# Fetching query and key blocks with fewer, wider DMAs, the first keys by halves, and a reordered start of a decoder layer on one core

## The chip, the core and the metric

The kernel runs on one core of one Trainium2 chip. The time is the device time of one execution in microseconds (us), the median of three runs. A core has TensorE (PE, matrix products), VectorE (DVE), ScalarE (ACT), GpSimd (POOL) and SyncE (SP), which here only issues DMAs. Each engine executes its instructions in its own fixed order, and waits for others by semaphores; an instruction that waits holds all that stand behind it. DMAs are issued by an engine's queue and carried out by 16 DMA engines.

## The reference, cut to what matters

One decoder layer in fp32 on x of shape (4, 1024, 256): self-attention, cross-attention on a context of 64 rows, and a feed-forward block with ternary weights, each behind a layer normalisation and with a residual. The change touches the self-attention alone:

```python
x = x + attn(layernorm(x))
# attn: 16 heads of width 16
q, k, v = split(x @ W_qkv + b_qkv)
energy = einsum('bqhe,bkhe->bqhk', q, k)
out = softmax(energy) / sqrt(256) @ v
out = out @ W_out + b_out
```

## The kernel before, in words

Self-attention is cut into 16 units: 4 batch rows of 1024 tokens, each with 4 groups of 4 heads. A unit takes the heads of its group in two pairs.

**Projection.** `ln1` (L324) normalises a batch's tokens and transposes them to xnT. `project(b, c)` (L341) makes q and k of half of the heads for one batch, in eight pieces of 256 columns (for the very first, four of 512). Each value is kept as two summands (a rounded part by ScalarE, L359, and the rest by VectorE, L360, together in a tile hl, of which there are two buffers), and each finished half of 512 tokens is written to device memory (kept_q, kept_k; 512 KB a write, L365).

**Fetch.** `fetch(u)` (L368) reads back what unit u needs. For each pair there is a tile q and a tile k of 128 partitions by 1024 tokens. The partitions hold, for each of two heads n, four blocks of 16 rows: for q the parts 0, 0, 1, 1 and for k the parts 0, 1, 0, 1, so that one product over 64 rows gives the sum of all four cross terms. `parts` (L380) issues one DMA for each block of 16 rows, so eight for a tile and 32 for a unit, on SP's queue. For unit 0, q comes in halves of 512 columns and four of the eight key blocks of each pair go by ScalarE's queue.

**Maxima and scores.** `maxima(u)` (L412) computes the energies once to find each row's maximum: for a tile of 128 queries, a pair and a half of the keys (kh), two matmuls into two banks of the ring of 7, then two VectorE reductions `mx` (L433). There are 64 reductions a unit. `turn_maxima` transposes them to mT. `scores` (L872) then computes the energies again, transposed, subtracts the maximum by a second matmul, and ScalarE takes the exponential (L888); `weigh` (L796) multiplies by v.

**Order.** The main loop (L891) has 16 steps a unit. A step issues scores of both pairs, two steps of the maxima (`top`), the weighing of the step before, and what `fill` picks from three lines of other work (`due`: layernorms, projections and values of later batches; `later`; `aside`), each with a number of pieces and a due time from which it gets credit. So the maxima run ahead: those of unit u+1 begin at step 6 of unit u, and need its second pair from the middle of step 7. Unit u+1 is fetched in steps 0 and 1 of unit u (L921 to L926), one pair a step. The maxima of the first half of unit 0 run ahead of the loop (L861), beside the values of batch 0 and the first two pieces of `project(0, 1)`. Ahead of them stands the start: x of batch 0 in four loads, wq and wk, the first layernorm, `project(0, 0)`, `fetch(0)`.

TensorE's matmuls and SP's DMAs are kept in program order (`ordered`, L54). For the other engines the framework's scheduler picks the order. In the first layernorm it puts VectorE's statistics of all eight token tiles (L233, L234) ahead of the first normalisation (L256).

Of the kernel before, what the change touches and what calls it, by code (L numbers as in the profile page):

```python
# [9 lines left out]
F32 = mybir.dt.float32  # L10
# [11 lines left out]
P = 128  # L22
# [8 lines left out]
def decoder_layer(ctx, tc, a, out):  # L31
# [24 lines left out]
    def matmul(*args, **kwargs):  # L56
        ordered(nc.tensor.matmul(*args, **kwargs))  # L57
# [4 lines left out]
    def dma(**kwargs):  # L62
        ordered(nc.sync.dma_start(**kwargs))
# [4 lines left out]
    x_of = {}  # L68
    x_slots = [const.tile([P, NT, E], F32, name=f"x{i}") for i in range(3)]

    def load_x(b, n=1, view=x_view, slot=None):
        step = NT // n
        x_of[b] = x_slots[b % 3 if slot is None else slot]
        for i in range(n):
# [20 lines left out]
    def load_row(name, cols=E):  # L95
        t = const.tile([P, cols], F32, name=name)
        nc.gpsimd.dma_start(out=t, in_=a[name].partition_broadcast(P))
        return t

    load_x(0, 4)  # L100
    wqk = []
    for name in ("wq", "wk"):

        wide = main.tile([P, E // P, H, 32], F32, tag="q", name=f"{name}_in", bufs=4)
        dma(out=wide, in_=a[name].rearrange("(c p) (h e) -> p c h e", p=P, e=32))
        t = const.tile([P, E // P, H, D], F32, name=name)
        nc.gpsimd.tensor_copy(t, wide[:, :, :, 1 : 1 + D])
        wqk.append(t.rearrange("p c h e -> p c (h e)"))
# [10 lines left out]
            )  # L119
        bqk[name] = t  # L120
    wv = load_w("wv", E, late=True)
    bo = load_row("bo")
    xbv = load_row("xbv")
    xbo = load_row("xbo")

    ident = const.tile([P, P], F32, name="ident")
    make_identity(nc, ident)
# [34 lines left out]
    for i in range(3):  # L162
        t = (const if i else main).tile([P, NT, VW], F32, tag=f"v_sb{i}", name=f"v_sb{i}")
        nc.gpsimd.memset(t, 16.0)
        v_sb.append(t)

    psum_stack = ctx.enter_context(ExitStack())
    ps = {}
# [9 lines left out]

    state = {"split": False, "banks": "ring"}

    def bank():
        return ps[state["banks"]]()
# [1 line left out]
    def two_banks():  # L186
        return [bank() for _ in range(2)]
# [41 lines left out]
    def ln_stats(pool, mv, blocks):  # L229

        for i, t in blocks:
            st = pool.tile([P, 6], F32, tag="bn", name="bn", bufs=3)
            nc.vector.bn_stats(out=st, in_=xs(t)[:, 0, :])  # L233
            nc.vector.bn_aggr(out=mv[:, i, :], in_=st)  # L234

    def ln_rstd(pool, rs, mv):
        n = mv.shape[1]
        sd = pool.tile([P, n], F32, tag="sd", name="sd", bufs=2)
        nc.scalar.activation(sd, mv[:, :, 1], AF.Sqrt, bias=eps_t[:, 0:1])
        nc.vector.reciprocal(out=rs, in_=sd)  # L240

    def ln_normalised(pool, mv, rs, i, t, n):
        xn = pool.tile([P, n, E], F32, tag="xn", name="xn", bufs=2)
        if state["split"]:
            nmr = pool.tile([P, n], F32, tag="nmr", name="nmr", bufs=2)
            nc.vector.scalar_tensor_tensor(
                nmr, mv[:, i : i + n, 0], -1.0, rs[:, i : i + n], ALU.mult, ALU.mult
            )
            for k in range(n):
                nc.scalar.activation(  # L250
                    xn[:, k, :], xs(t + k)[:, 0, :], AF.Identity, bias=nmr[:, k : k + 1],
                    scale=rs[:, i + k : i + k + 1],
                )
            return xn
        for k in range(n):
            nc.vector.tensor_scalar(  # L256
                xn[:, k, :], xs(t + k)[:, 0, :], mv[:, i + k, 0:1], rs[:, i + k : i + k + 1],
                ALU.subtract, ALU.mult,
            )
        return xn  # L260

# [106 lines left out]
    def fetch(u):  # L368

        b, g = divmod(u, NG)  # L370
        pairs = qk_of[u] = []
        rest = []
        for pair in range(2):
            q = main.tile([P, S], F32R, tag="q", name="q", bufs=4)
            k = main.tile([P, S], F32R, tag="k", name="k", bufs=4)
            pairs.append((q, k))
            kept_q, kept_k = split_of[b, g // 2]
            f0 = 64 * (g % 2) + 32 * pair

            def parts(t, kept, order, n, cols, issue, f0=f0):  # L380
                for i, part in enumerate(order):
                    r, f = 64 * n + 16 * i, f0 + 16 * n
                    issue(out=t[r : r + 16, cols].bitcast(F32), in_=kept[part, f : f + 16, cols])

            if u:
                halves = (slice(0, S),)
            else:
                halves = (slice(0, 512), slice(512, S))
            for n in range(2):
                parts(q, kept_q, (0, 0, 1, 1), n, halves[0], dma)  # L390
            for n in range(2):
                parts(k, kept_k, (0, 1, 0, 1), n, slice(0, S), dma if u or n else nc.scalar.dma_start)
            for n in range(2):
                for cols in halves[1:]:
                    rest.append((parts, q, kept_q, (0, 0, 1, 1), n, cols, dma))
            if pair:
                for f, *args in rest:
                    f(*args)
            yield

    def values(b):
        for i in range(NT):
            yield "cols+"
            pv = bank()[:, 0:E]
            tokens = slice(i * P, (i + 1) * P)
            product(pv, [(xnT_of[b][:, c, tokens], wv[:, c, :]) for c in range(2)])
            nc.scalar.copy(  # L407
                v_sb[b % 3][:, i, 0 : H * 17].rearrange("p (h e) -> p h e", e=17)[:, :, 1:17],
                pv.rearrange("p (h e) -> p h e", h=H),
            )  # L410

    def maxima(u):  # L412


        mx = main.tile([P, NT, NG, 2], F32, tag="mx", name="mx", bufs=2)
        m_of[u] = []
        for half in range(2):
            order = [(t, pair) for t in range(half * 4, half * 4 + 4) for pair in range(2)]
            if u == 0 and half == 0:

                order.sort(key=lambda at: at[1])
            for t, pair in order:
                q, k = qk_of[u][pair]
                for kh in range(2):
                    sides = two_banks()
                    for n, pm in enumerate(sides):
                        r = slice(64 * n, 64 * n + 64)
                        matmul(
                            pm, lhsT=q[r, t * P : (t + 1) * P],
                            rhs=k[r, kh * 512 : (kh + 1) * 512], start=True, stop=True,  # L430
                        )
                    for n, pm in enumerate(sides):
                        nc.vector.tensor_reduce(  # L433
                            mx[:, t, 2 * pair + n : 2 * pair + n + 1, kh], pm, AX.X, ALU.max
                        )
                    if kh == 1 and (t, pair) == order[-1]:
                        turning.append(turn_maxima(u, mx[:, half * 4 : half * 4 + 4, :, :]))
                    yield

    def turn_maxima(u, mx):  # L440
        nm = main.tile([P, 4, NG], F32, tag="nm", name="nm", bufs=2)
# [385 lines left out]
        next(parts)  # L827
    run(first)
    run(parts)
    state["split"] = True  # L830
    run(fetch(0))

    sel_f = post_pool.tile([P, 2, P], F32, tag="xn", name="sel_f", bufs=2)
# [22 lines left out]
    begun = {}  # L856


    due.add(values(0), 8)
    due.add(project(0, 1), 8)  # L860
    for i in range(16):  # L861
        top()
        if i % 3 != 0 and i < 15:
            due.step()
    run(turning.popleft())
    due.credit = 0.0
    load_x(1)
    loading = late_loads()

# [21 lines left out]
    for u in range(NU):  # L891
# [272 lines left out]
```

## Time and profile before

| what | value |
|---|---|
| runs | 1366.59 us median of 3 (1365.82 to 1367.46) |
| the profiled execution | 1365.17 us, of which the span from first to last instruction 1363.4 us |
| busy: TensorE, VectorE, ScalarE | 1282.1, 1004.7, 898.5 us |
| mean granted TensorE clock | 0.979 of full speed |
| DMA, mean over the span | 53 GB/s, 72.72 MB |
| k and q fetch issues | 248 + 240 DMAs of 64 KB and 32 of 32 KB on SP, 8 of 64 KB on ScalarE |
| first exponentials of unit 0, and of unit 15's end | 60.4 us and 1098.0 us |

The profile follows one execution. Its page lists the busy time of each engine, then a map of the span in 40 slices, then the DMA queues, then the chain of work that ended last (followed back from the last instruction, each step to what released it), then groups of instructions with count, busy time and mean duration, with the idle time ahead of them and what ended it. Single stretches can be asked for: the busy time of each engine in a stretch with the granted clock (PEclk, 1.00 is full), the DMA engines' mean busy share and the bytes a second; one engine's instructions in order of time; and the DMA packets of a stretch with their share of the 16 engines. PE is TensorE's matmuls, PEld its weight loads, SPq a DMA issue by SP. All times of the profile count from the start of the span. Attention is the stretch from about 58 to 1098 us, some 64 us a unit; the feed-forward block follows.

### The profile page before, as it was taken

To read this page: it belongs to the slowest core of one execution; us is meant where nothing else is said; L and a number is where in the kernel's file an instruction comes from. 1 tells how busy PE (TensorE), PEld (TensorE's weight loads), DVE (VectorE), ACT (ScalarE), POOL (GpSimd) and SP (SyncE) were. 2 spreads that over 40 slices of the span, in tenths; PEclk is the share of its full clock that TensorE was granted. 3 is DMA by queue.
4 is the path that set the end of the run, shared out by engine and by line. 5 is a ranking of instruction groups with operands and counts; after the bars stand their busy time and mean duration, and the time that the engine had idled before them with its cause. 6 is when DMAs were issued, how large, how long until landed. Compare 5 with 4: busy or idle time off the path is not lost.

```text
span 1363.4 us, 27651 instructions
## 1 busy us (share of the span) xinstructions
PE 1282.1 (94%) x11000; PEld 717.4 (53%) x11000; DVE 1004.7 (74%) x2110; ACT 898.5 (66%) x1654; POOL 80.0 (6%) x86
## 2 busy tenths in 40 slices
PE   3879999999999999999999999999999988999987
PEld 1434445545545454444545544545455466776777
DVE  4877777867878877877877777878889357565665
ACT  1377666756687667777676676676766746474765
POOL 4000000003010000011000000010000012000000
PEclk9889999999999999989999999999999989999989
DMA  5440312312130202131212112212210010100000
GB/s 169 126 143 30 111 42 68 94 48 63 41 85 1 63 7 57 33 93 31 64 35 60 38 27 75 82 53 73 55 40 1 2 62 1 44 19 31 1 31 32
DMA packets 46064, 72.72 MB, mean 53 GB/s; under 512 B 11280, under 2 KB 27920, under 8 KB 45936
## 3 DMA queue, kind: packets, MB, share of 16 engines
q1 hardware_dynamic: 44720, 68.47, 17.0%
q8 instruction: 87, 1.43, 0.4%
q10 hardware_dynamic: 1072, 2.10, 0.4%
q0 software_dynamic: 144, 0.39, 0.2%
q14 instruction: 41, 0.34, 0.1%
HBM read 46.81 MB, written 24.12 MB: 52 GB/s over the span
## 4 chain that ended last, share of the span: by engine, by line
PE 73%; DVE 16%; ACT 8%; issue 2%; DMA 1%; SPq 0%; DVEq 0%; ACTq 0%
PE ps_ring L57 42%; PE ps_acc L57 15%; PE ps_wide L57 8%; DVE mx L433 8%; PE ps_misc L57 3%; ACT exp L888 3%; PE ps_misc L60 2%; PE ps_ring L60 2%; DVE nm L592 2%; ACT xn L250 1%; DVE xn L256 1%; DVE bn L233 1%; DMA x<-in_x 1%; ACT ex L625 1%; ACT hl L359 1%
## 5 line engine op out<-in xcount | busy, mean ns | idle before, releaser
L433 DVE TENSOR_REDUCE mx<-ps_ring 128x1 f32<-128x512 f32 x1024 | 646.4, 682 | 157.6 <-PE ps_ring L57 156.7
L888 ACT ACTIVATE exp<-ps_ring 128x512 f32<-128x512 f32 x1024 | 549.2, 606 | 191.1 <-PE ps_ring L57 187.5
L57 PE MATMUL ps_ring<-q,k 64*128 64x512 f32 x1024 | 280.5, 474 | 8.0 <-ACT exp L888 5.9
L57 PE MATMUL ps_ring<-k,q 64*128 64x512 f32 x1024 | 260.2, 425 | 20.1 <-DMA q<-kept_q 7.9
L57 PE MATMUL ps_acc<-exp,v_sb 128*32 128x512 f32 x2048 | 275.3, 610 | 0.0
L57 PE MATMUL ps_ring<-mT,sel 64*128 64x512 f32 x1024 | 232.8, 400 | 0.2 <-ACT mT L451 0.2
L57 PEld LDWEIGHTS ps_ring<-q,k 64*128 64x128 f32 x1024 | 115.5, 185 | 198.4 <-ACT exp L888 69.0
L57 PEld LDWEIGHTS ps_ring<-k,q 64*128 64x128 f32 x1024 | 124.2, 186 | 100.2 <-ACT exp L888 41.3
L57 PEld LDWEIGHTS ps_ring<-mT,sel 64*128 64x128 f32 x1024 | 108.0, 186 | 6.3 <-ACT mT L451 0.7
L57 PEld LDWEIGHTS ps_acc<-exp,v_sb 128*32 128x32 f32 x2048 | 40.5, 108 | 67.4 <-issue 65.6
L1004 DVE BATCH_NORM_STATS2 bnh<-h 128x6 f32<-128x512 f32 x64 | 41.2, 679 | 34.1 <-ACT h L1001 34.0
L1001 ACT ACTIVATE h<-ps_wide 128x1024 f32<-128x1024 f32 x32 | 32.7, 1026 | 41.6 <-PE ps_wide L57 41.5
L1036 DVE SCALAR_TENSOR_TENSOR hl<-ps_misc,lnw,hT 128x512 fp32r<-128x512 f32 x64 | 46.4, 733 | 18.2 <-ACT hT L1035 18.2
L57 PE MATMUL ps_wide<-wproj,hl 128*128 128x256 f32 x256 | 46.2, 303 | 12.6 <-DVE hl L1036 12.5
L57 PE MATMUL ps_wide<-wfc,xl 128*128 128x512 f32 x128 | 56.5, 442 | 1.4 <-DVE xl L271 1.4
L57 PE MATMUL ps_wide<-wfc,xh 128*128 128x512 f32 x128 | 54.3, 424 | 0.0
L1035 ACT ACTIVATE hT<-ps_misc,lnw 128x512 fp32r<-128x512 f32 x64 | 42.6, 687 | 16.3 <-PE ps_misc L60 16.3
L233 DVE BATCH_NORM_STATS2 bn<-x 128x6 f32<-128x256 f32 x96 | 38.8, 416 | 8.1 <-DMA x<-in_x 6.4
L57 PEld LDWEIGHTS ps_wide<-wproj,hl 128*128 128x128 f32 x256 | 34.9, 191 | 16.2 <-DVE hl L1036 14.8
L280 POOL TENSOR_TENSOR x<-x,xbo 128x512 f32<-128x512 f32 x16 | 20.6, 1295 | 367.0 <-ACT xn L250 358.5
L57 PE MATMUL ps_wide<-wproj,hT 128*128 128x256 f32 x256 | 41.4, 284 | 0.0
L407 ACT COPY v_sb<-ps_ring 128x256 f32<-128x256 f32 x32 | 12.0, 375 | 41.0 <-PE ps_ring L57 30.6
(166 smaller groups left out, 1467.1 us busy)
## 6 DMA issues: line engine op xcount, KB each, us to landing
k<-kept_k SPq DMA_DIRECT2D x248, 64.0 KB
q<-kept_q SPq DMA_DIRECT2D x240, 64.0 KB
kept_q<-hl SPq DMA_DIRECT2D x15, 512.0 KB
kept_k<-hl SPq DMA_DIRECT2D x14, 512.0 KB
out<-x SPq DMA_DIRECT2D x16, 256.0 KB
x<-in_x SPq DMA_DIRECT2D x3, 1024.0 KB
x_kept<-x SPq DMA_DIRECT2D x3, 1024.0 KB
x<-x_kept SPq DMA_DIRECT2D x3, 1024.0 KB
```

The source lines that it names most:

```text
L57: ordered(nc.tensor.matmul(*args, **kwargs))
L60: ordered(nc.tensor.transpose(*args))
L233: nc.vector.bn_stats(out=st, in_=xs(t)[:, 0, :])
L250: nc.scalar.activation(xn[:, k, :], xs(t + k)[:, 0, :], AF.Identity, bias=nmr[:, k : k + 1], scale=rs[:, i + k : i + k + 1],)
L280: nc.gpsimd.tensor_tensor(xs(t, 2), xs(t, 2), row.rearrange("p (o d) -> p o d", o=1).to_broadcast([P, 2, E]), ALU.add,)
L433: nc.vector.tensor_reduce(mx[:, t, 2 * pair + n : 2 * pair + n + 1, kh], pm, AX.X, ALU.max)
L592: nc.vector.tensor_reduce(nm[:, t, s, :], pm[s].rearrange("p (h k) -> p h k", k=SK), AX.X, ALU.max, negate=True,)
L888: nc.scalar.activation(ex[:, n, :], pe[n], AF.Exp)
L1001: nc.scalar.activation(h[:, t, :], ph.rearrange("p a f -> p (a f)"), AF.Gelu)
L1004: nc.vector.bn_stats(out=st[:, half, :], in_=h[:, t, half * 512 : (half + 1) * 512])
L1035: nc.scalar.activation(hT, pt, AF.Copy, scale=w)
L1036: nc.vector.scalar_tensor_tensor(hl, pt, w, hT.bitcast(F32), ALU.mult, ALU.subtract)
```

## The change

Six things are edited.

1. The first load of x is cut: two of four pieces, then wq, then the other two, then wk. The three row broadcasts bo, xbv and xbo (issued by GpSimd) move from before the constants to behind the memsets of v_sb.
2. While the start runs, VectorE's layernorm instructions are kept in program order (`pinned`), so each half of the tokens is normalised before the statistics of the next.
3. `parts` joins blocks of 16 rows by two: one DMA writes 32 partitions. For q the source is one part repeated by a broadcast, for k both parts. A unit has 16 DMAs of 128 KB in place of 32 of 64 KB.
4. For unit 0 the keys are fetched by halves of 512 columns too, and the maxima of its first four query tiles go through the first half of the keys before the second (sorted by pair, then kh, then tile).
5. The first four of eight pieces of `project(0, 1)` are issued right behind `fetch(0)`, ahead of all maxima; the loop ahead of the main loop takes the eight pieces of `values(0)` alone, one in every second turn.
6. `fetch(1)` is issued as a whole ahead of the load of x for batch 1 and of the late weights. The load of x for batch 2 moves from the start of unit 0 to step 2 of unit 1.

```diff
-    load_x(0, 4)
+    load_x(0, 4, parts=(0, 1))
     for name in ("wq", "wk"):
...
+        if name == "wq":
+            load_x(0, 4, parts=(2, 3))
...
+    def pinned(ins):
+        if state["pinned"]:
+            ordered(ins)
...
-            nc.vector.bn_stats(out=st, in_=xs(t)[:, 0, :])
-            nc.vector.bn_aggr(out=mv[:, i, :], in_=st)
+            pinned(nc.vector.bn_stats(out=st, in_=xs(t)[:, 0, :]))
+            pinned(nc.vector.bn_aggr(out=mv[:, i, :], in_=st))
...
             def parts(t, kept, order, n, cols, issue, f0=f0):
-                for i, part in enumerate(order):
-                    r, f = 64 * n + 16 * i, f0 + 16 * n
-                    issue(out=t[r : r + 16, cols].bitcast(F32), in_=kept[part, f : f + 16, cols])
+                r, f = 64 * n, f0 + 16 * n
+                for i in (0, 2):
+                    part = order[i]
+                    if order[i + 1] == part:
+                        src = kept[part : part + 1, f : f + 16, cols]
+                        src = src.to_broadcast([2, *src.shape[1:]])
+                    else:
+                        src = kept[:, f : f + 16, cols]
+                    issue(out=t[r + 16 * i : r + 16 * i + 32, cols].bitcast(F32), in_=src)
...
-            for n in range(2):
-                parts(k, kept_k, (0, 1, 0, 1), n, slice(0, S), dma if u or n else nc.scalar.dma_start)
+            for cols in halves:
+                for n in range(2):
+                    parts(k, kept_k, (0, 1, 0, 1), n, cols, dma if u or n else nc.scalar.dma_start)
...
-                order.sort(key=lambda at: at[1])
+                order.sort(key=lambda at: at[1:])
...
-    due.add(project(0, 1), 8)
+    parts = project(0, 1)
+    for _ in range(5):
+        next(parts)
+    due.add(values(0), 8)
+    due.add(rest_of(parts), 4)
     for i in range(16):
         top()
-        if i % 3 != 0 and i < 15:
+        if i % 2 == 0:
             due.step()
...
+    run(fetch(1))
     load_x(1)
...
-                if n > 1:
+                if n > 2:
                     load_x(n)
...
+            if u == 1 and step == 2:
+                load_x(2)
-            if step < 2 and u + 1 < NU:
+            if step < 2 and 0 < u < NU - 1:
```

More of the change, by code (lines that the diff above doesn't have):

```diff
@@ L69, in decoder_layer, with load_x @@
     x_slots = [const.tile([P, NT, E], F32, name=f"x{i}") for i in range(3)]
-    def load_x(b, n=1, view=x_view, slot=None):
+    def load_x(b, n=1, view=x_view, slot=None, parts=None):
         step = NT // n
         x_of[b] = x_slots[b % 3 if slot is None else slot]
-        for i in range(n):
+        for i in parts or range(n):
             sl = slice(i * step, (i + 1) * step)
@@ L121, in decoder_layer @@
     wv = load_w("wv", E, late=True)
-    bo = load_row("bo")
-    xbv = load_row("xbv")
-    xbo = load_row("xbo")
     ident = const.tile([P, P], F32, name="ident")
@@ L165, in decoder_layer @@
         v_sb.append(t)
+    bo = load_row("bo")
+    xbv = load_row("xbv")
+    xbo = load_row("xbo")
     psum_stack = ctx.enter_context(ExitStack())
@@ L175, in decoder_layer @@
     open_psum("ring", 7, [P, 512])
-    state = {"split": False, "banks": "ring"}
+    state = {"split": False, "banks": "ring", "pinned": True}
+    def pinned(ins):
+        if state["pinned"]:
+            ordered(ins)
     def bank():
@@ L239, in ln_rstd @@
         nc.scalar.activation(sd, mv[:, :, 1], AF.Sqrt, bias=eps_t[:, 0:1])
-        nc.vector.reciprocal(out=rs, in_=sd)
+        pinned(nc.vector.reciprocal(out=rs, in_=sd))
     def ln_normalised(pool, mv, rs, i, t, n):
@@ L255, in ln_normalised @@
         for k in range(n):
-            nc.vector.tensor_scalar(
-                xn[:, k, :], xs(t + k)[:, 0, :], mv[:, i + k, 0:1], rs[:, i + k : i + k + 1],
-                ALU.subtract, ALU.mult,
+            pinned(
+                nc.vector.tensor_scalar(
+                    xn[:, k, :], xs(t + k)[:, 0, :], mv[:, i + k, 0:1], rs[:, i + k : i + k + 1],
+                    ALU.subtract, ALU.mult,
+                )
             )
@@ L417, in maxima @@
         for half in range(2):
-            order = [(t, pair) for t in range(half * 4, half * 4 + 4) for pair in range(2)]
+            order = [
+                (t, pair, kh) for t in range(half * 4, half * 4 + 4) for pair in range(2) for kh in range(2)
+            ]
             if u == 0 and half == 0:
-                order.sort(key=lambda at: at[1])
-            for t, pair in order:
+                order.sort(key=lambda at: at[1:])
+            for at in order:
+                t, pair, kh = at
                 q, k = qk_of[u][pair]
[L424 to L438, printed above, removed]
+                sides = two_banks()
+                for n, pm in enumerate(sides):
+                    r = slice(64 * n, 64 * n + 64)
+                    matmul(
+                        pm, lhsT=q[r, t * P : (t + 1) * P],
+                        rhs=k[r, kh * 512 : (kh + 1) * 512], start=True, stop=True,
+                    )
+                for n, pm in enumerate(sides):
+                    nc.vector.tensor_reduce(
+                        mx[:, t, 2 * pair + n : 2 * pair + n + 1, kh], pm, AX.X, ALU.max
+                    )
+                if at == order[-1]:
+                    turning.append(turn_maxima(u, mx[:, half * 4 : half * 4 + 4, :, :]))
+                yield
     def turn_maxima(u, mx):
@@ L829, in decoder_layer @@
     run(parts)
-    state["split"] = True
+    state.update(split=True, pinned=False)
     run(fetch(0))
@@ L856, in decoder_layer, with rest_of @@
     begun = {}
+    parts = project(0, 1)
+    for _ in range(5):
+        next(parts)
+    def rest_of(gen):
+        yield "cols+"
+        yield from gen
     due.add(values(0), 8)
-    due.add(project(0, 1), 8)
+    due.add(rest_of(parts), 4)
     for i in range(16):
         top()
-        if i % 3 != 0 and i < 15:
+        if i % 2 == 0:
             due.step()
```

## The prediction, on record before the changed kernel ran

> **What bounds the kernel now.** I read the page first (busy times, chain), then the stretches by engine, then SP's timeline and the DMA view in single stretches.
>
> ```profile
> PE 1282.1 (94%) x11000; PEld 717.4 (53%) x11000; DVE 1004.7 (74%) x2110; ACT 898.5 (66%) x1654; POOL 80.0 (6%) x86
> PE 73%; DVE 16%; ACT 8%; issue 2%; DMA 1%; SPq 0%; DVEq 0%; ACTq 0%
> ```
>
> TensorE carries the span, and the chain that ended last holds 1% of DMA: behind the front no transfer is late. The stretches say where TensorE does wait.
>
> ```profile
> core 0: us, PE busy (x) PEld busy (x) DVE busy (x) ACT busy (x) POOL busy (x), PEclk, DMA share, GB/s
> ...
> 28.00:34.00 6.00, 0.00 (x0) 0.00 (x0) 0.00 (x0) 0.00 (x0) 0.00 (x0) 0.66 0.71 221
> 34.00:41.00 7.00, 6.84 (x50) 2.79 (x54) 4.21 (x7) 0.75 (x2) 0.00 (x0) 0.56 0.48 120
> ...
> 88.00:98.00 10.00, 4.12 (x22) 1.55 (x26) 5.06 (x14) 6.72 (x11) 0.00 (x0) 0.50 0.67 212
> ```
>
> From 28 to 34 us every engine waits for the first fetch, and from 86.6 to 93.9 TensorE waits for the second; the granted clock (second last but one column) is near half in and after each. A later unit has nothing of the kind:
>
> ```profile
> 448.00:476.00 28.00, 27.65 (x244) 13.94 (x242) 22.30 (x48) 19.38 (x39) 0.00 (x0) 1.00 0.29 77
> ```
>
> So a fetch is hidden there. By how much? SP's timeline for unit 7's fetch, and the DMA view from 448 to 465 us:
>
> ```profile
> 448.05 3.54 SPq L63 DMA_DIRECT2D q<-kept_q  x8
> 451.63 4.67 SPq L63 DMA_DIRECT2D k<-kept_k  x8
> 456.40 3.60 SPq L63 DMA_DIRECT2D q<-kept_q  x8
> 460.05 3.67 SPq L63 DMA_DIRECT2D k<-kept_k  x8
> ```
> ```profile
> DMA packets 1026, 2.12 MB, mean 125 GB/s; under 512 B 512, under 2 KB 512, under 8 KB 1024
> q1 hardware_dynamic: 1024, 2.10, 45.9%
> ```
>
> 32 DMAs carry 512 packets of 4 KB and 512 tiny ones: 16 completions for each DMA, that is, each runs on 16 engines. They cost 0.459 x 17 us x 16 = 125 engine-us, spread over 16 engines in 17 us. Counting 64 mx reductions to a unit, unit 7's first (the 449th) starts at 476.3 and the first that needs its second pair (the 453rd) at 481.4, 33.4 us after the fetch's first issue. Over units 2 to 15 that lead is 29.6 to 37.1, mean 33.4; the matmul stands 1 us ahead of its reduction, so **a fetch has about 32.4 us**.
>
> **The merged fetch decides.** The diff's words don't say it, but `parts` is rewritten: two DMAs of 16 rows become one of 32, whose source now leads with a dimension of 2 (stride 0 where the part is repeated, the part dimension otherwise) against 32 partitions in SBUF. 32 DMAs of a unit become 16. An issue lasts 0.46 us (3.67/8), so SP is spared 7 us a unit; SP is idle from 463.7 to 508.9, so this is worth 0.
>
> Two rules of the Trainium skill, "DMA: Bandwidth & Descriptors", face each other. "Rules for kernel authors" wants small transfers joined; that supports the change, at 0 as just said. "Why a DMA increments its semaphore by 16 and not by 1" says that the engine count is the largest k up to 16 that divides the slowest dimension other than 1 of both sides, and that these are the lowest-numbered engines: here k = 2, always the same two. Does the trace agree? One load of before has this shape, xbk (source 2 x 32, destination 32 partitions). The DMA view of 74.6 to 75.05 us holds one of them:
>
> ```profile
> DMA  0000000001100000000021221110010100000000
> ...
> DMA packets 66, 0.00 MB, mean 1 GB/s; under 512 B 66, under 2 KB 66, under 8 KB 66
> ...
> xbk<-in_xbk SPq DMA_DIRECT2D x1, 0.2 KB
> ```
>
> 64 elements and 2 completions, against 16 in the fetches; and the busy share stands at 1 to 2 tenths (2 of 16 engines is 0.125). So k = 2 is measured. That it is always the same two, no row shows: I take it from the page.
>
> A packet's cost has two ends. The fetch's own row: 125 engine-us, on two engines 62.4 us. The row nearest to what two full queues do, packets back to back, is the tail of the wfc load, 932.1 to 933.1 us:
>
> ```profile
> DMA packets 96, 0.39 MB, mean 393 GB/s; under 512 B 0, under 2 KB 0, under 8 KB 96
> q1 hardware_dynamic: 96, 0.39, 96.8%
> ```
>
> 0.968 x 16 / 96 = 161 ns a packet; 256 for each engine = 41.2 us. In the fetches of before a packet finds its engine idle, since an engine gets one per 0.46 us; in the new ones it queues. That idle start seems to be the dear part: the first fetch's 2 KB packets cost 160 ns (the DMA view of 41 to 46 us: 29.7% of 16 engines, 148 packets), the 4 KB ones 244, so the second 2 KB cost 84. I take 41.2 and keep 62.4 for the range. The first packet moves 0.9 us after the issue (the empty slices at the DMA row's start), so the fetch ends 42.1 us after it began: **9.7 us late** (slow end: 30.9). The matmul waits in TensorE's order, and behind it scores, weighing and so exp and the reductions. Units 2 to 15: 14 x 9.7 = **136 us** (slow end 433).
>
> **Clock after each stall.** Before's waits of 8 and 7 us left the clock at half for about 6 us (34 to 40) and 4 us (94 to 98) of work: a loss of 2 to 3 us. 14 x 2.5 = **35 us** (0 if the idle stays too short, 42 at most).
>
> **Writes and loads behind the fetch.** SP issues in order, and in the built order each DMA first waits for the landing of the eighth before it; so SP is held about 21 us instead of 15, and a kept write queued behind a fetch has its share on the two full engines, landing after 43 us. hl has two buffers: the third tile's activation on ACT waits for the first one's write, with all exps behind it. Unit 3 has its tiles at steps 1-2, 3-4, 5-6 and 7-8; the third would be due at 22 us (7.5 steps take 33.4), and stops to about 46: 24 instead of 10, **+14**. In the other units I find the third tile after step 7.5, or the write between the pairs. The two engines' share of writes (16 packets of 2 KB, 1.5 us) and x loads (64 of 1 KB at 58 ns, as in 1100.3 to 1104.5: 3.7 us) that fall into leads: some six, **+10** (0 to 25).
>
> **The front.** Taken alone its parts gain. (a) The chain spends 7.36 us on x with the first half's statistics done at 5.4; in order, and with wq ahead of two x pieces and of the three row broadcasts, transposes start near 7 instead of 11.5, but wk and the second half follow: -4 (0 to -5). (b) Keys by halves: the chain has 8 us from the last k piece (26.05) to the first compare (34.17); the first half can go before the last write: -2 (0 to -4). (c) Half of project(0,1), 4 pieces of 1.06 us, goes into 28 to 34, so 2 leave the compare loop (VectorE: 2 x 0.47) and the clock stays up (34 to 41 at 0.56): -2; and 2 leave the TensorE-bound loop: -2. Their two writes queue on SP behind fetch(0), in front of fetch(1). (d) fetch(1) before x1: TensorE's 7.2 us and the cold clock after it: -6 (0 to -9). x2, moved behind fetch(2), is first read by VectorE near unit 2's first reductions; steps 3 to 7 of unit 1 hide it with 16 engines, with two it lands 3.7 us behind fetch(2), within the +10. Sum -16.
>
> With two engines this turns over. fetch(0) is 32 DMAs of 64 KB: 16 packets of 2 KB for each engine at half of the 161 ns, 1.3 us each, 41 us in all; from about 17 us to 59. Its first 24 are enough for the compare loop, which so ends near 56 (57.0 before). fetch(1) follows, to about 101, and x1's share on the two engines to about 105. In the built order x1's statistics stand on VectorE ahead of the 59th reduction, step 4 of unit 0; they hold all reductions until then. The compare of unit 1's second pair, 3.5 steps of 4.4 us on, comes at about 121; before 101.2. **+20** (-10 to +35), the gains included.
>
> **Sum.** 136 + 35 + 14 + 10 + 20 = +215. The profiled execution took 1365.2 (span 1363.4, 1.8 around it), 1.4 under the median 1366.6: 1366.6 + 215 = **1582 us**.
>
> **Rivals.** (1) Two engines, packets as slow as the fetch's own: 433 + 35 + 14 + 10 + 40, about 1900. For: the same tensors and rows; against: those packets never queued. Between the two ends anything can lie.
> (2) *Faster*: the pairs of engines rotate (or the rule fails). Eight DMAs in flight on two engines each fill 16, a fetch again takes about 17 us, and the front's -16 remains: about 1350. It decides from the point where a fetch fits in 32.4 us, that is from 2.6 engines (82.4/31.5) on. For: no row shows which engines; against: the page names the lowest-numbered.
> (3) The same two engines, but leads stretch: with the clock down or other waits inside the lead, a stall of 5 instead of 9.7 and no lost clock: 14 x 5 + 14 + 10 + 10, about 1470.
>
> **Chances.** Forecast 62%, rival (1) and what lies between 20%, (3) 7%, (2) 11%. Of (2), one in ten ends within 0.2%, about what this measurement can tell from no change. Slower 0.88, same 0.02, faster 0.10. Range: 1480 leaves (2) and part of (3) out, about 14%; 1820 leaves the slowest out, 6%.
>
> **What would show it.** k = 2: completions per unit's fetch drop from 512 to 32, with 512 packets of 4 KB kept. Same two engines: the fetch's data takes 41 us or more, its busy share sits near 0.125, and SP's second eight issues are paced by landings. Stalls: in each unit a TensorE idle of about 10 us until q or k, ahead of its first second-pair reductions, with PEclk at half behind it, and DMA as a large share of the chain. Front: transposes at 7 us, work between 26 and 32, and VectorE waiting for x1 to about 105. If fetches end within 20 us, the main step is wrong and (2) holds; if packets take 240 ns, (1).

## The result, and the profile after

The changed kernel took **1618.96 us** (median, 1618.49 to 1619.43), against 1366.66 us beside it: a ratio of 1.185, with a 95% interval of 1.183 to 1.187. The forecast was 1582 us, in a range of 1480 to 1820. The direction and the mechanism hold; of +252 us it found +215.

The page of the changed kernel first: busy times, then the chain that ended last, by engine and by line.

```profile
PE 1321.6 (82%) x11000; PEld 728.4 (45%) x11000; DVE 1004.8 (62%) x2110; ACT 897.7 (56%) x1654; POOL 78.8 (5%) x86
...
PE 43%; DMA 33%; SPq 11%; DVE 7%; ACT 5%; issue 2%; DVEq 0%; ACTq 0%
PE ps_ring L57 21%; DMA k<-kept_k 20%; SPq L63 11%; PE ps_acc L57 9%; PE ps_wide L57 7%; DMA q<-kept_q 5%; DMA x<-in_x 3%; PE ps_misc L57 3%; PE ps_misc L60 2%; DVE mx L452 2%; ACT exp L916 2%; DMA kept_k<-hl 1%; DMA kept_q<-hl 1%; DMA raw<-in_wproj 1%; DMA raw<-in_wfc 1%
```

TensorE executes the same 11000 matmuls. VectorE and ScalarE are as busy as before, TensorE 40 us more (its mean granted clock is 0.903 of full speed, 0.979 before), and the span is 254 us longer: what was added is mostly waiting. The chain says for what. DMA rises from 1% to 33%, and SP's issues, which wait for earlier DMAs, from 0 to 11%.

One unit's fetch, SP's timeline (start, duration, engine, line, operation, tiles, count), then the DMA view of 566.3 to 610 us:

```profile
566.34 2.46 SPq L63 DMA_DIRECT2D q<-kept_q  x4
568.85 4.35 SPq L63 DMA_DIRECT2D k<-kept_k  x4
573.29 10.32 SPq L63 DMA_DIRECT2D q<-kept_q  x4
583.66 9.85 SPq L63 DMA_DIRECT2D k<-kept_k  x4
```
```profile
DMA  0111111111111111111111111111111111111110
...
DMA packets 547, 2.14 MB, mean 49 GB/s; under 512 B 32, under 2 KB 32, under 8 KB 544
...
q1 hardware_dynamic: 544, 2.10, 12.1%
```

544 packets are 512 of data and 32 completions: two a DMA, so two engines. The busy share stays at one tenth while eight DMAs are in flight: were the pairs to rotate, eight would fill all 16. The packets cost 0.121 x 43.7 us x 16 / 512 = 165 ns each (161 was put in), and the data ends 43.2 us after the first issue (42.1).

TensorE's timeline of the same fetch's end; in brackets stands the wait ahead of the instruction and what ended it:

```profile
598.39 0.72 PE L57 MATMUL ps_ring<-mT,sel 64*128 64x512 f32 x2
604.85 0.76 PE L57 MATMUL ps_ring<-k,q 64*128 64x512 f32 x1 [5.74 <-DMA k<-kept_k]
609.98 0.76 PE L57 MATMUL ps_ring<-k,q 64*128 64x512 f32 x1 [4.37 <-DMA k<-kept_k]
```

5.74 + 4.37 = 10.1 us of waiting (9.7 forecast), in two pieces, since the two heads' keys land one after the other. The same place in the stretches by engine, whose third last column is the granted clock:

```profile
570.00:597.00 27.00, 26.74 (x256) 13.35 (x252) 22.35 (x51) 17.70 (x34) 0.00 (x0) 1.00 0.13 53
597.00:606.00 9.00, 2.87 (x19) 1.49 (x19) 2.76 (x8) 2.62 (x6) 0.00 (x0) 0.78 0.13 53
606.00:612.00 6.00, 2.02 (x9) 0.48 (x9) 1.03 (x2) 0.00 (x0) 0.00 (x0) 0.50 0.07 27
612.00:645.00 33.00, 32.90 (x288) 17.87 (x286) 24.34 (x45) 21.08 (x41) 0.00 (x0) 0.94 0.02 6
```

TensorE is full until 597, waits, and resumes at half clock. Then the front, where 28 to 34 us was empty before and 34 to 41 was not:

```profile
28.00:34.00 6.00, 5.68 (x69) 2.53 (x67) 2.56 (x5) 2.11 (x4) 0.00 (x0) 0.95 0.41 160
34.00:41.00 7.00, 2.48 (x17) 0.88 (x17) 1.10 (x2) 0.00 (x0) 0.00 (x0) 0.60 0.22 83
88.00:98.00 10.00, 5.23 (x50) 2.77 (x46) 2.87 (x5) 5.08 (x10) 0.00 (x0) 0.94 0.13 52
98.00:118.00 20.00, 0.00 (x0) 0.00 (x0) 0.50 (x2) 0.00 (x0) 0.00 (x0) 0.50 0.31 91
```

The early projection does fill 28 to 34, but from 98 to 118 TensorE stands still. Who holds it is seen in the waits of the whole run (engine, tile and line, what it waits for: total us, times, longest):

```profile
PE ps_ring L57 <- DMA k<-kept_k: 107.4, 21, 11.8
...
DVE bn L241 <- DMA x<-in_x: 51.7, 4, 25.9
ACT hl L369 <- DMA kept_q<-hl: 26.8, 2, 23.2
DVE part L757 <- DMA raw<-in_wfc: 23.2, 1, 23.2
DVE part L757 <- DMA raw<-in_wproj: 22.1, 1, 22.1
```

Beside the keys there are five single waits of over 20 us: four of VectorE's, for x of batches 1 and 2 and for the two raw weights of the feed-forward block, and one of ScalarE's for a kept write. All four loads and the write stand on SP's queue behind a fetch.

For the sums below I cut the span at the first exponential of each unit (us; "start" is what lies ahead of unit 0, "rest" what follows the last exponential):

| kernel | start | units 0 to 15 | rest |
|---|---|---|---|
| before | 60.4 | 73.4 63.4 58.6 67.5 66.3 62.0 62.4 64.7 69.1 65.1 66.5 67.5 66.3 64.4 62.2 58.1 | 265.4 |
| the change | 72.9 | 91.4 90.1 70.7 88.7 79.2 77.0 75.3 76.5 83.2 74.5 78.1 75.9 84.5 89.3 86.3 58.1 | 265.6 |
| unjoined_2_engines | 69.7 | 90.2 84.7 71.4 77.9 78.5 76.4 75.1 76.4 83.4 74.3 78.0 77.9 83.6 80.7 75.1 58.1 | 265.3 |
| join_late_readers | 70.9 | 92.9 84.5 75.0 88.9 78.4 77.3 75.3 76.5 87.7 69.2 78.5 74.7 91.0 78.0 76.5 56.0 | 265.3 |
| join_16_leads | 56.9 | 64.6 65.3 55.9 64.5 66.2 62.0 62.1 64.7 70.1 65.1 66.5 67.5 66.3 65.8 63.0 58.1 | 265.8 |

Units 5, 6, 7, 9, 10 and 11, with little or nothing else behind their fetch, are 15.0, 12.9, 11.8, 9.4, 11.6 and 8.4 us longer after the change than before, mean 11.5. TensorE's waits ahead of the first compares with new keys (those of over 1 us, summed by unit) are, in these six, 12.6, 10.1, 9.1, 7.1, 9.3 and 6.1 us, mean 9.1. The other 2.4 us match TensorE's busy time, which for the same work is 2.3 to 2.9 us longer in each of the six, mean 2.5, as the granted clock is lower behind the wait. Unit 15, which fetches nothing, and the feed-forward block are unchanged.

### The profile page after: what moved, and what is told of

The parts are those of the page before. It is cut to its first block, busy times and chain, and to the rows that moved or that the text cites. A ratio compares the mean times of both kernels' runs of the same rounds, so it can differ in the third digit from the quotient of the medians.

```text
span 1617.3 us, 27390 instructions
## 1 busy us (share of the span) xinstructions
PE 1321.6 (82%) x11000; PEld 728.4 (45%) x11000; DVE 1004.8 (62%) x2110; ACT 897.7 (56%) x1654; POOL 78.8 (5%) x86
## 3 DMA queue, kind: packets, MB, share of 16 engines
q1 hardware_dynamic: 37056, 68.44, 11.6%
## 4 chain that ended last, share of the span: by engine, by line
PE 43%; DMA 33%; SPq 11%; DVE 7%; ACT 5%; issue 2%; DVEq 0%; ACTq 0%
PE ps_ring L57 21%; DMA k<-kept_k 20%; SPq L63 11%; PE ps_acc L57 9%; PE ps_wide L57 7%; DMA q<-kept_q 5%; DMA x<-in_x 3%; PE ps_misc L57 3%; PE ps_misc L60 2%; DVE mx L452 2%; ACT exp L916 2%; DMA kept_k<-hl 1%; DMA kept_q<-hl 1%; DMA raw<-in_wproj 1%; DMA raw<-in_wfc 1%
## 5 line engine op out<-in xcount | busy, mean ns | idle before, releaser
L57 PE MATMUL ps_ring<-k,q 64*128 64x512 f32 x1024 | 272.5, 436 | 190.4 <-DMA k<-kept_k 107.4
L57 PE MATMUL ps_acc<-exp,v_sb 128*32 128x512 f32 x2048 | 285.7, 631 | 0.0
L57 PEld LDWEIGHTS ps_ring<-k,q 64*128 64x128 f32 x1024 | 128.4, 192 | 278.2 <-issue 135.8
L369 ACT ACTIVATE hl<-ps_ring,bk_c 128x256 fp32r<-128x256 f32 (+1 forms) x30 | 14.6, 489 | 106.0 <-PE ps_ring L57 61.9
L57 PEld LDWEIGHTS ps_acc<-exp,v_sb 128*32 128x32 f32 x2048 | 41.0, 110 | 70.9 <-issue 69.0
L1066 DVE SCALAR_TENSOR_TENSOR hl<-ps_misc,lnw,hT 128x512 fp32r<-128x512 f32 x64 | 46.4, 732 | 18.2 <-ACT hT L1065 18.2
L57 PE MATMUL ps_wide<-wproj,hl 128*128 128x256 f32 x256 | 46.2, 303 | 12.6 <-DVE hl L1066 12.5
L1031 ACT ACTIVATE h<-ps_wide 128x1024 f32<-128x1024 f32 x32 | 32.7, 1026 | 42.1 <-PE ps_wide L57 42.0
L370 DVE SCALAR_TENSOR_TENSOR hl<-ps_ring,bk_c,hl 128x256 f32<-128x256 f32 (+1 forms) x30 | 14.9, 500 | 57.5 <-ACT hl L369 57.5
L57 PEld LDWEIGHTS ps_wide<-wproj,hl 128*128 128x128 f32 x256 | 34.9, 191 | 16.2 <-DVE hl L1066 14.8
```

Of the source, the lines that this page charges most:

```text
L370: nc.vector.scalar_tensor_tensor(hl[:, 1, part], pq, bias, hl[:, 0, part], ALU.add, ALU.subtract)
L1031: nc.scalar.activation(h[:, t, :], ph.rearrange("p a f -> p (a f)"), AF.Gelu)
L1066: nc.vector.scalar_tensor_tensor(hl, pt, w, hT.bitcast(F32), ALU.mult, ALU.subtract)
```

## The experiments

All ratios are against the kernel before, with the 95% interval.

### Is it the joined fetch, and in it the two engines?

**join_alone**: the kernel before, with the change's `parts` and nothing else.

> The kernel before with the joined DMAs of the change and nothing else. Theory 1: nearly the whole of the change's loss, some 12 us in each of units 2 to 14, more where a load queues behind a fetch and VectorE waits for it, and the front without its gains: about 1615 us (1580 to 1650). Theory 2: about 1366 us.

Measured: 1622.3 us, 1.1875 (1.1859 to 1.1891). The joined fetch alone costs as much as all edits together.

**unjoined**: the change with the 32 DMAs of before.

```diff
-                for i in (0, 2):
-                    part = order[i]
...
-                    issue(out=t[r + 16 * i : r + 16 * i + 32, cols].bitcast(F32), in_=src)
+                for i, part in enumerate(order):
+                    r, f = 64 * n + 16 * i, f0 + 16 * n
+                    issue(out=t[r : r + 16, cols].bitcast(F32), in_=kept[part, f : f + 16, cols])
```

> The change with the old parts: one DMA for each block of 16 rows again, all else as in the change. Theory 1 (the joined DMAs run on two engines, always the same, and that is what costs): the fetch again takes about 17 us, the stalls of units 1 to 14 go, and the front's gains stay, so about 1350 us (1340 to 1362). Theory 2 (the new order of the front and the early second fetch cost, by what they push back on SP): it stays above 1500. Theory 3 (a DMA of 128 KB is what is slow, whatever its engines): 1350 as well, told apart by join_16_leads.

Measured: 1360.0 us, 0.9952 (0.9939 to 0.9966). A gain, but 10 us less than expected. Its first exponential comes at 63.5 us, later than before's 60.4: keys by halves double the first fetch's key DMAs, and SP issues that fetch until 51.5 us (46.7 before). The second fetch follows, so x of batch 1 is issued only at 70.0.

**unjoined_4_engines** and **unjoined_2_engines**: the same 32 DMAs and the same bytes, but the 16 rows of each described as 4 x 4, or 2 x 8, so that the slowest dimension is 4 or 2.

```diff
-                    issue(out=t[r : r + 16, cols].bitcast(F32), in_=kept[part, f : f + 16, cols])
+                    src = kept[part, f : f + 16, cols].rearrange("(b a) t -> a b t", a=4)
+                    issue(out=t[r : r + 16, cols].bitcast(F32), in_=src)
```

> As unjoined, but the 16 rows of a block are taken in the order 0, 4, 8, 12, 1, ... so that a dimension of 4 leads the source: each DMA runs on four engines (the row order is the same in q and k). Theory 1 with the lead as its threshold: 512 packets of 161 ns on four engines take 20.6 us, inside the 32.4 us that a fetch has, so no stall in the later units; only the front, where fetch(0) and fetch(1) are waited for, loses some 5 to 10 us against unjoined: 1350 to 1368. If instead any slower fetch costs in proportion (no threshold), half of the two engines' loss is seen: near 1480.

Measured: 1359.8 us, 0.9956 (0.9943 to 0.9968), the same as with 16 engines. The DMA view of one fetch (443 to 466.5 us) shows that the four engines are real:

```profile
DMA  0011321221322122222222222222222222223222
...
DMA packets 624, 2.09 MB, mean 89 GB/s; under 512 B 122, under 2 KB 122, under 8 KB 620
```

About 120 completions are four to a DMA, and the share is about two tenths (4 of 16 is 0.25). The fetch lasts some 24 us instead of 17, inside the lead of 32.4, and costs nothing. Between four engines and two lies a threshold, not a slope. The 5 to 10 us that I expected the front to lose did not show: the start is 2.6 us shorter than unjoined's and unit 0 is 3.6 longer (60.9 and 69.0 against 63.5 and 65.4).

> As unjoined_4_engines, with a dimension of 2 in front: 32 DMAs of 64 KB a unit, each on two engines. Theory 1: the two engines alone make the loss, the joining has no part in it: 41.2 us of packets a fetch as in the change, so 1600 to 1640, about 1620 us. Theory 3 (the 128 KB DMA or its repeated source is slow): near unjoined's 1360.

Measured: 1577.1 us, 1.1548 (1.1532 to 1.1565), 43 us less than I expected. Its ordinary units (76.4, 75.1, 76.4 for units 5 to 7) are within 0.6 us of the change's: with the number and size of DMAs of before, two engines alone make the stall. That the two kernels are 42 us apart is in units 1 (5.4), 3 (10.8), 13 (8.6), 14 (11.2) and the start with unit 0 (4.4); this is taken up below.

**join_16_leads**: the change with the same 16 DMAs of 128 KB, only the two source dimensions changed over, so that 16 leads and 2 follows. Every instruction keeps its place on every engine.

```diff
                     if order[i + 1] == part:
-                        src = kept[part : part + 1, f : f + 16, cols]
-                        src = src.to_broadcast([2, *src.shape[1:]])
+                        src = kept[part : part + 1, f : f + 16, cols].rearrange("l p t -> p l t")
+                        src = src.to_broadcast([16, 2, src.shape[2]])
                     else:
-                        src = kept[:, f : f + 16, cols]
+                        src = kept[:, f : f + 16, cols].rearrange("l p t -> p l t")
```

For q, each of the 16 rows then stands twice in succession, and for k the two parts alternate row by row. The sum over a head's 64 rows still has the same four cross terms, in another order.

> The change with the same 16 joined DMAs of 128 KB a unit, the same instructions in the same order on every engine, but the 16 rows lead in the source and the two copies or parts come second, so that the rows of a block alternate in q and k alike (the sum over rows is the same). Theory 1: 16 divides both leading sizes, each DMA has 16 completions instead of 2, a fetch takes about 10 to 17 us, about 1350 us (1338 to 1362). Theory 3: as slow as the change, 1600 to 1620.

Measured: **1350.3 us, 0.9882** (0.9869 to 0.9896), faster than both kernels. The DMA view of one fetch (431.8 to 448 us):

```profile
DMA  0008369488637794674885820172882000000000
...
DMA packets 769, 2.11 MB, mean 131 GB/s; under 512 B 256, under 2 KB 256, under 8 KB 768
```

The same 512 data packets, now with 256 completions, 16 a DMA, and over in about 11 us. So between 1619 and 1350 us stands only the order of two dimensions in the source of these DMAs, and with it the order of the rows in q and k.

**join_16_on_before**: this form of `parts` in the kernel before.

> The kernel before with joined DMAs whose 16 rows lead, nothing else. In the change's front this form against the old one was worth 9.7 us (1360.0 to 1350.3); here fetch(1) stands behind two loads of x, so less of it can show: about 1360 us (1354 to 1366). If the front's gain of 16 us were all the joining's and none the reordering's, 1350.

Measured: 1357.6 us, 0.9946 (0.9932 to 0.9960). Halving the DMAs is worth 8.2 us here, and 9.7 us in the change (1360.0 to 1350.3); in the change nearly all of it is in the start and units 0 and 3 (63.5, 65.4 and 67.2 us in unjoined, 56.9, 64.6 and 64.5 in join_16_leads).

### Why single units lose 10 to 15 us more than the stall

**loads_by_pool**: the change, with the loads of x for batches 1 and 2 and of the two raw weights issued by GpSimd, past SP's queue.

```diff
-    load_x(1)
+    load_x(1, issue=nc.gpsimd.dma_start)
...
-                load_x(2)
+                load_x(2, issue=nc.gpsimd.dma_start)
...
-        dma(
+        nc.gpsimd.dma_start(
             out=flat.rearrange("p (c f) -> p c f", c=w.shape[1]),
```

> The change with the loads of x for batches 1 and 2 and of the two feed-forward weights issued by GpSimd instead of SP, so that they don't queue behind a fetch[...]. Theory: what the sum missed is VectorE's in-order wait for those loads (units 0, 1, 13 and 14 cost 6, 14, 13 and 12 us more than the other units' 12): about 40 us less, near 1575 us (1555 to 1595). Rival (the loads only overlap stalls that the fetches make anyway, and the long units have another cause): 1610 to 1622.

Measured: 1591.3 us, 1.1654 (1.1635 to 1.1673): 28 us of the 44 expected. Units 0, 1, 13 and 14 gain 5.5, 9.0, 5.3 and 13.6 us. But the start loses 5.3: VectorE now meets the statistics of x of batch 1 there, ahead of the last pieces of the first projection, waits for the load, and so the write of the second half of kept_k is issued at 34.97 us instead of 30.61. In unit 13 the load of wfc has landed (1111.17) before the fetch begins, but it delays the kept write that the fetch waits for, and the fetch's first issue comes 4.1 us into the unit instead of at its start. What stands behind a fetch is a cost of its own, and moving the transfer only partly removes it.

I first took unjoined_2_engines' 42 us for a shorter queue: eight DMAs of 64 KB in flight hold what stands behind them half as long as eight of 128 KB. The traces contradict that. The raw weights (wfc) land 46.6 us after the fetch's first issue in the change (1118.02 to 1164.65) and 46.4 us in unjoined_2_engines (1097.53 to 1143.9); x of batch 2 48.8 and 47.8 us. What differs is where the reader stands. VectorE's timeline, the change:

```profile
1140.22 1.27 DVE L452 TENSOR_REDUCE mx<-ps_ring 128x1 f32<-128x512 f32 x2
1164.68 1.28 DVE L757 TENSOR_REDUCE part<-raw 128x1 f32<-128x512 f32 x2 [23.18 <-DMA raw<-in_wfc]
1165.87 0.68 DVE L452 TENSOR_REDUCE mx<-ps_ring 128x1 f32<-128x512 f32 x1
```

and unjoined_2_engines:

```profile
1137.22 0.69 DVE L447 TENSOR_REDUCE mx<-ps_ring 128x1 f32<-128x512 f32 x1 [9.36 <-PE ps_ring L57]
1142.33 0.69 DVE L447 TENSOR_REDUCE mx<-ps_ring 128x1 f32<-128x512 f32 x1 [4.42 <-PE ps_ring L57]
1143.91 1.28 DVE L752 TENSOR_REDUCE part<-raw 128x1 f32<-128x512 f32 x2 [0.89 <-DMA raw<-in_wfc]
```

In the first, the row sums of the raw weights stand ahead of unit 13's 63rd reduction, that is, ahead of six reductions that need no new keys; VectorE stops for 23 us, the ring of 7 banks fills, and TensorE waits 24.0 us for a reduction. In the second they stand behind unit 14's sixth, so behind the stall for the keys, which covers them. The framework's scheduler chose both places.

**join_late_readers**: the change, fetches as they are, with the readers later. To hold them there the edit keeps the reductions of the maxima in program order too, so other places on VectorE and ScalarE move with them.

```diff
-            pinned(nc.vector.bn_stats(out=st, in_=xs(t)[:, 0, :]))
+            keep = ordered if t // NT in (1, 2) else pinned
+            keep(nc.vector.bn_stats(out=st, in_=xs(t)[:, 0, :]))
...
-                    nc.vector.tensor_reduce(
+                    ordered(nc.vector.tensor_reduce(
...
-            yield "free"
-            nc.vector.tensor_reduce(
+            for _ in range(1 if i else 5):
+                yield "free"
+            ordered(nc.vector.tensor_reduce(
...
-            aside.add(ternary("wfc", 2, HID), 10)
-            aside.add(ternary("wproj", HID // P, E), 10)
+            aside.add(ternary("wfc", 2, HID), 14)
+            aside.add(ternary("wproj", HID // P, E), 14)
```

> The change with its two-engine fetches as they are; only the place of three readers on VectorE moves: the statistics of x for batches 1 and 2 and the maxima are kept in program order, so that x2's statistics stand ahead of unit 3's 13th reduction in place of unit 2's third, and the row sums of the raw feed-forward weights stand ahead of unit 14's 13th and unit 15's 37th reduction in place of unit 13's 63rd and unit 14's 61st. SP's order is the same. Reason: in the change and in the unjoined fetch on two engines these loads land equally long after the fetch's first issue (raw wfc 46.6 and 46.4 us, x2 48.8 and 47.8), and yet VectorE waits 22 to 23 us for them in the one and about 1 us in the other, whose order has the readers behind the reductions that wait for the fetch itself. Theory, the place of the readers: units 1, 13 and 14 lose what they lost there, 5, 9 and 11 us, up to all of what they have above an ordinary unit (15, 13, 13); units 3 and the front stay; about 1594 (1580 to 1600), and no wait for raw or x2 of over 3 us. Rival, the loads' own time behind the fetch (its backlog of 128-KB DMAs, their share of the two engines): moving the readers frees nothing, 1612 to 1622.

Measured: 1596.9 us, 1.1679 (1.1651 to 1.1706): 22 us less than the change, near the theory's 1594 and clear of the rival's 1612. The waits for raw and for x of batch 2 are gone. TensorE's timeline near the end of unit 13, in the change:

```profile
1166.61 0.79 PE L57 MATMUL ps_ring<-k,q 64*128 64x512 f32 x1 [23.96 <-DVE mx L452]
```

and in join_late_readers, where only the ordinary wait for the keys is left, 12.3 us:

```profile
1158.34 0.76 PE L57 MATMUL ps_ring<-k,q 64*128 64x512 f32 x1 [8.08 <-issue]
1163.36 0.76 PE L57 MATMUL ps_ring<-k,q 64*128 64x512 f32 x1 [4.26 <-DMA k<-kept_k]
```

By unit the picture is less clean: units 12 to 14 together lose 14.6 us (+6.5, -11.3, -9.8), units 1 and 2 only 1.3 (-5.6, +4.3), and units 8 and 9, where no reader was to move, change by +4.5 and -5.3. So the place of the readers is shown as a cause for the raw weights; for x of batch 2 its wait went, and most of the time came back in the next unit. Unit 3 stays at 88.9: its wait is ScalarE's for a kept write, which lands 44.9 us after the fetch's first issue in the change and 44.7 in unjoined_2_engines, where the waiting activation stands 12 exponentials later. That this accounts for its 10.8 us is read from the order and was not tried.

### The gains of the front, one by one

Each kernel is join_16_leads with one edit undone. All of them undone at once is join_16_on_before, which is 7.3 us slower than join_16_leads (1357.6 and 1350.3). A single figure below is thus what one edit is worth beside the other three, good to about 2 us (the runs of join_16_leads alone span 1348.5 to 1352.2).

**join_16_late_fetch**: `fetch(1)` behind x of batch 1 and in steps again, x of batch 2 at unit 0 again.

```diff
-    run(fetch(1))
...
-                if n > 2:
+                if n > 1:
                     load_x(n)
...
-            if u == 1 and step == 2:
-                load_x(2)
-            if step < 2 and 0 < u < NU - 1:
+            if step < 2 and u + 1 < NU:
```

> join_16_leads with fetch(1) back in unit 0's first two steps, behind the load of x for batch 1 and with that for batch 2 ahead of it again. Step (d) of the prediction priced the early fetch(1) at 6 us (0 to 9): about 1356 us (1350 to 1360).

Measured: 1355.4 us, 0.9924 (0.9911 to 0.9936): undoing step (d) alone costs 5.1 us (6 forecast).

**join_16_old_start**: x in one run of four loads, broadcasts early, VectorE's order free.

```diff
-    load_x(0, 4, parts=(0, 1))
+    load_x(0, 4)
...
-    state = {"split": False, "banks": "ring", "pinned": True}
+    state = {"split": False, "banks": "ring", "pinned": False}
```

> join_16_leads with the old start: four loads of x in a row, the row broadcasts ahead of the constants, VectorE's first layernorm in the scheduler's order. Step (a) of the prediction: 4 us (0 to 5) lost, about 1354 us. The trace of the change puts the first write of q at 15.0 instead of 19.9 us, so up to 1355.

Measured: 1354.3 us, 0.9916 (0.9901 to 0.9930): undoing step (a) alone costs 4.0 us (4 forecast).

**join_16_whole_keys**: unit 0's keys fetched and compared whole.

```diff
-            for cols in halves:
-                for n in range(2):
-                    parts(k, kept_k, (0, 1, 0, 1), n, cols, dma if u or n else nc.scalar.dma_start)
+            for n in range(2):
+                parts(k, kept_k, (0, 1, 0, 1), n, slice(0, S), dma if u or n else nc.scalar.dma_start)
...
-                order.sort(key=lambda at: at[1:])
+                order.sort(key=lambda at: at[1])
```

> join_16_leads with unit 0's keys fetched whole and its first maxima in the old order. Step (b): 2 us (0 to 4) lost, about 1352 us. Rival: the halves double the key DMAs of unit 0 (8 to 16), and whole keys are no slower: 1348 to 1350.

Measured: 1354.2 us, 0.9913 (0.9895 to 0.9931): undoing step (b) alone costs 3.9 us (2 forecast).

**join_16_late_proj**: `project(0, 1)` not begun beside the fetch.

```diff
-    parts = project(0, 1)
-    for _ in range(5):
-        next(parts)
...
     due.add(values(0), 8)
-    due.add(rest_of(parts), 4)
+    due.add(project(0, 1), 8)
...
-        if i % 2 == 0:
+        if i % 3 != 0 and i < 15:
```

> join_16_leads without the early half of project(0, 1): all eight pieces follow the values, in the old order of the loop ahead of the main one. Step (c): 4 us lost (2 in that loop, 2 in the main loop), about 1354 us, with the granted clock down again in the first compares. Rival (VectorE bounds that loop, so TensorE's pieces and clock don't matter there): only the 2 us of the main loop, 1352.

Measured: 1358.0 us, 0.9940 (0.9928 to 0.9953): undoing step (c) alone costs 7.7 us (4 forecast), as much as all four together.

## Why the prediction was right, and where its sum was short

Regrouped by the forecast's own terms, from the table of units (after less before):

| term | forecast | measured |
|---|---|---|
| 14 stalls with their lost clock | 136 + 35 = 171 | 14 x 11.5 = 161 |
| the front: start and unit 0 | 20 | 12.5 + 18.0 = 30.5 |
| writes and loads behind a fetch | 14 + 10 = 24 | 62 |
| sum | 215 | 254 |

The last term is what units 1 to 4, 8 and 12 to 14 have above the 11.5: 15.2 (1), 0.6 (2), 9.7 (3), 1.4 (4), 2.6 (8), 6.7, 13.4 and 12.6 (12 to 14).

- **Two engines, always the same.** Right, and the step on which all else stood: 2 completions a DMA, a flat share of 0.13, and join_16_leads, where only the dimension order differs. That it is always the same pair shows in the share, which stays at one tenth with eight DMAs in flight; which pair, no row shows. What the Trainium skill states ("DMA: Bandwidth & Descriptors", "Why a DMA increments its semaphore by 16 and not by 1") holds for k = 2, 4 and 16. Rival (2), about 1350, is what join_16_leads measures, once the fetch has its 16 engines.
- **The packet's cost.** 161 ns taken from a full queue; 165 measured. Rival (1), at the 244 ns that the same packets took on idle engines, fell. So the row to read was that of the new condition (a full queue), not that of the same tensors.
- **The stall.** 9.7 us forecast, 10.1 measured at unit 7's keys; over the six ordinary units 6.1 to 12.6, mean 9.1. Clock 2.5 forecast, some 2.4 measured. Stall and clock together 12.2 forecast, 11.5 measured. Rival (3) fell.
- **The front, 10 us short.** Gains (a) to (d) were summed to 16, and 16 us separate before from join_16_leads (1366.3 to 1350.3), but that agreement is luck. The four edits together are worth 6.3 us with the old DMAs (1366.3 to 1360.0) and 7.3 us with the joined ones (1357.6 to 1350.3); undone singly they sum to 20.7, so each needs the others and single prices can't be added. The other 8 to 10 us belong to the halved issue count, which the forecast put at 0: SP is idle in a later unit, but not in the front. The loss was under-sized. The step said that the first fetch runs to 59 us and x of batch 1 lands at 105. In the chain of the change stand the write of the second half of kept_k, a write of the next projection, and the load of x of batch 1:

```profile
30.61 8.60 DMA kept_k<-hl
...
62.35 10.18 DMA kept_k<-hl
...
98.15 19.33 DMA x<-in_x
```

  The first of them was issued at 26.05 us before and took 3.04; it has a share on the two engines that the fetch fills. SP's first group of key issues takes 19.00 us, of which 10.2 go to the landing of a q block and 6.1 to this write. The first fetch is over only near 72, and x, issued at 98.15 behind eight fetch DMAs in flight, lands at 117.5. VectorE waits 25.95 us for it. The forecast had priced writes behind a fetch for unit 3 and not for the front.
- **Writes and loads behind the fetch: the failed step.** The forecast took for each load "the two engines' share", 3.7 us, and for x of batch 2 "it lands 3.7 us behind fetch(2), within the +10". It lands 48.8 us after the fetch's first issue, 5 to 6 behind the fetch's end, so the transfer was roughly right. What failed is the reader: VectorE meets it in order, ahead of reductions that could still run, and stops 22 to 23 us, so that TensorE stands 21 to 24 us in units 1, 13 and 14 instead of about 10. That is a wait, 13 to 15 us a load, where a transfer share was booked. Moving the readers takes 22 us off the whole, of which units 1, 2 and 12 to 14 show 16, against the 41 that units 1, 13 and 14 had above the 11.5. Unit 3's +14 was near (9.7). Unit 12's 6.7 and what remains of unit 1 were not traced to one cause.

## What to carry to other kernels

Before joining small DMAs, look at the slowest dimension on both sides: it sets how many engines carry one, and completions per DMA in the packet counts show it. A transfer's price depends on whether it still fits its lead: four engines cost nothing here, two cost 217 us with 32 DMAs a unit (1360.0 to 1577.1). When a transfer gets later, list every in-order reader of whatever is queued behind it, and ask what stands behind that reader; what it holds up is the price, not its own bytes.

## What the runs showed of the hardware

- DMAs of k = 2 don't spread over further engines with eight of them in flight: together they move 52 GB/s, 26 GB/s an engine, flat for 40 us. The same 2.1 MB take about 42 us on two engines, 24 on four and 11 on 16 with joined DMAs.
- The mean cost of a 4-KB packet, completions included, falls with the number of packets that one DMA gives to an engine: 244 ns for one (before), 216 for two (join_16_leads, 42.7% of 16 engines in 16.2 us), 177 for four (unjoined_4_engines, 23.4% in 23.5 us, 498 packets), 165 for 16 (the change). That the first packet after a pause is the dear one, as the forecast took it, fits this and was not tested apart; the number of engines at work differs too.
- A load of 1 MB that uses other engines too takes 19 to 20 us from issue to landing behind eight DMAs of 128 KB on two engines (19.33, 20.24, 19.29 and 19.51 us in the chain). An estimate for what stands ahead of it on each of the two: 128 packets at 165 ns, 21 us.
- After a TensorE wait of 10 us in two pieces, the granted clock is 0.50 in the 6 us that hold its end (606 to 612 us) and 0.94 over the next 33.
